# Cross-attention block on one core: the causal mask of the first two pairs laid by TensorE, and the first keys ahead of the first queries

## Chip, core and metric

The kernel runs on one core of a Trainium2 chip. The metric is the device time of one execution in microseconds. The kernel before takes 1587.69 us (median of three runs, 1587.53 to 1588.26). Engines are named as the profile names them: PE is TensorE (its weight loads are PEld), DVE is VectorE, ACT is ScalarE, POOL is GpSimd, SP is the engine that issues most DMAs. An "ACTq" or "SPq" in a view is the instruction queue of that engine where it issues a DMA.

## What is computed

For 128 sequences of 128 tokens and 256 features, in float32: queries come from `x`, keys and values from a context `c`; 16 heads of width 16; a strictly causal mask (key j is allowed for query i only if j < i); softmax; the first row of the attention set to zero; an output projection; a layer norm over the residual; a two-layer network with a hidden width of 1024 and ReLU; a second layer norm.

```python
q = (query @ Wq + bq) ; k = (key @ Wk + bk) ; v = (values @ Wv + bv)   # split into 16 heads
scores = einsum('bhqd,bhkd->bhqk', q, k) / sqrt(16)
scores = where(j < i, scores, -1e30)
attn = softmax(scores) ; attn[:, :, 0, :] = 0
x = layer_norm(query + (attn @ v) @ Wo + bo, ln1_g, ln1_b)
out = layer_norm(x + relu(x @ W1 + b1) @ W2 + b2, ln2_g, ln2_b)
```

## The kernel before

Two sequences make a pair, and 64 pairs go through the same stages. The order of instructions on each engine is written out by hand (`tc.manual_schedule`, L59): each call of a helper appends its instructions to the queues of the engines it uses, and an engine works through its queue in that order, waiting where an operand or a buffer isn't ready. `step(p)` (L799) writes the order for pair p in the middle of the kernel; the order for pairs 0 and 1 stands by itself, in L681 to L784, and there the work of these two pairs is interleaved.

The stages of a pair that matter here:

- `tokens` (L242) or, for pairs 0 and 1, `transposed` (L220) brings x and c into a layout with features on the partitions. For pairs 0 and 1 this is four TensorE transposes each, against the identity, into one bank of PSUM, which VectorE (pair 0, L689) or ScalarE (pair 1, L730) copies out.
- `queries` and `keys` (L266, L276) multiply with Wq and Wk (four matmuls of 128x128 by 256 columns) and are emptied from PSUM by ScalarE with bias and scale. Keys are written twice, once for each half of a 32-row strip (`half`, `bkh`). For pair 0 the keys are written out at L703 to L721: two banks, one emptied by ScalarE, one by VectorE.
- `scores(p, hi)` (L316): 64 small matmuls of 32 rows by 64 columns of weights. The 128 queries are split into a high half, which sees 128 keys, and a low half, which sees 64. Results stand in two tiles of two banks each, from a pool that holds two such tiles (`ps_2`, L72), so four banks in all: the next scores can be written only when the ones before have been read.
- `mask(p, hi, t)` (L340): VectorE adds the mask `neg` (0 or -1e30) to one of the two tiles and writes the sum to SBUF (`sm`). `maximum` (L352): VectorE takes the row maximum, and GpSimd subtracts it. `exponential` (L362) is ScalarE. `sums` (L368): VectorE sums and inverts, GpSimd scales.
- `turn_on_pe` (L410), for pairs 0 and 1: TensorE transposes the probabilities, four 128x128 blocks to a bank, and ScalarE copies each bank to `pT`. From pair 2 on this is done by VectorE (`turn`) and DMAs (`bring`).
- `weigh`, `context`, `attention_out`, `attention_sum`, `attention_stats`, `norm1`: probabilities times values (`pc`), output projection (`po`), residual and layer norm. `norm1(0)` is followed by TensorE transposes (`ptn`) and the hidden layer (`ph`, `py`).
- Single banks (`bank`, L213) come from a pool of four (`ps_1`, L73).

At the start, loads are issued by SP and ACT in the order of L126 to L159: the first x, Wq, Wk, Wv and so on by SP, the first c and the small bias columns by ACT. GpSimd makes the identity (L139) and the mask `neg` (L166 to L172). TensorE runs twelve transposes of the identity that nothing reads (`warm`, L681 to L683) until the first x has landed.

Of the kernel before, what the change touches and what calls it, by code (L numbers as in the profile page):

```python
# [19 lines left out]
def tile_cross_attention_block(  # L20
# [76 lines left out]
    def load_tokens(g, us=slice(0, 4)):  # L97
        if g not in tokens_of:
            tokens_of[g] = loads.tile([P, 4, D], F32, tag="x", name=f"x_{g}", bufs=2)
        nc.sync.dma_start(  # L100
            tokens_of[g][:, us], x[4 * g + us.start : 4 * g + us.stop].rearrange("b p d -> p b d")
        )


    def weight(w, name):
        n = w.shape[0] // P
        t = const.tile([P, n, w.shape[1]], F32, tag=name, name=name)
        nc.sync.dma_start(t, w.rearrange("(k p) n -> p k n", p=P))
        return t

    def column(v, name):
        t = const.tile([P, v.shape[1]], F32, tag=name, name=name)
        nc.scalar.dma_start(t, v)
        return t
# [9 lines left out]
        return t  # L124

    load_tokens(0, slice(0, 2))  # L126
    wq = weight(Wq, "wq")
    c_first = const.tile([P, 4, D], F32, tag="c_first", name="c_first")
    nc.scalar.dma_start(c_first[:, 0:2], c[0:2].rearrange("b p d -> p b d"))
    bq_c = column(bq, "bq_c")  # L130
    bk_c = column(bk, "bk_c")
    wk = weight(Wk, "wk")
    wv = weight(Wv, "wv")
    load_tokens(0, slice(2, 4))
    nc.sync.dma_start(c_first[:, 2:4], c[2:4].rearrange("b p d -> p b d"))
# [77 lines left out]
    def bank(name):  # L213
        return ps_1.tile([P, 512], F32, tag="ps1", name=name)

    def pair(name):
        return ps_2.tile([P, 2, 512], F32, tag="ps2", name=name)
# [24 lines left out]
    def tokens(p, which):  # L242
        st = states.setdefault(p, {})
        st[which + "T"] = proj.tile([P, KC, TP], F32, tag=which + "T", name=f"{which}T_{p}")
        nc.vector.transpose(
            st[which + "T"], blocks_of.pop((which, p)).rearrange("p k u f -> p k (u f)")
        )
# [18 lines left out]
    def queries(p):  # L266
        st = states[p]
        st["qT"] = proj.tile([P, KC, TP], F32, tag="qT", name=f"qT_{p}")
        pq = project(wq, st["xT"], f"pq_{p}")
        for m in range(KC):  # L270
            nc.scalar.activation(  # L271
                st["qT"][:, m, :], pq[:, m * TP : (m + 1) * TP], AF.Identity,
                bias=bqs_c[:, m : m + 1], scale=QSCALE,
            )

    def keys(p):  # L276
        st = states[p]
        st["kT"] = proj.tile([P, KC, 2, TP], F32, tag="kT", name=f"kT_{p}")
        pk = project(wk, st["cT"], f"pk_{p}")
        for m in range(KC):  # L280
            for e in range(2):
                nc.scalar.activation(  # L282
                    st["kT"][:, m, e, :], pk[:, m * TP : (m + 1) * TP], AF.Identity,
                    bias=bkh[:, m, e : e + 1], scale=half[:, e : e + 1],
                )
# [27 lines left out]

    def scores(p, hi):  # L316

        st = states[p]
        n = P if hi else HP
        sps = [pair(f"pss{hi}_{p}_{t}") for t in range(2)]  # L320
        for m in range(KC):
            for s in range(2):
                first = s * P
                for r in range(NS):
                    strip = slice(32 * r, 32 * r + 32)
                    nc.tensor.matmul(  # L326
                        sps[r // 2][
                            s * HP : (s + 1) * HP, r % 2, m * 2 * n : (m + 1) * 2 * n
                        ].rearrange("p (e j) -> p e j", e=2),
                        st["qT"][strip, m, first + hi * HP : first + hi * HP + HP],  # L330
                        st["kT"][strip, m, :, first : first + n],
                        start=True, stop=True,
                    )
        st["sps", hi] = sps
        st["sm", hi] = soft.tile(
            [P, H, n], F32, tag=f"sm{hi}", name=f"sm{hi}_{p}", bufs=2
        )
        st["nmx", hi] = small.tile([P, H], F32, tag=f"nmx{hi}", name=f"nmx{hi}_{p}")

    def mask(p, hi, t):  # L340
        st = states[p]
        part = slice(t * HH, (t + 1) * HH)
        n = P if hi else HP
        no = neg.rearrange("p u j -> p (u j)") if hi else neg[:, 1, :]
        nc.vector.tensor_tensor(  # L345
            st["sm", hi][:, part, :].rearrange("p (r n) j -> p r n j", r=2),
            st["sps", hi][t][:, :, : 4 * n].rearrange("p r (n j) -> p r n j", j=n),
            no[:, None, None, :].to_broadcast([P, 2, 4, n]),
            ALU.add,
        )  # L350

    def maximum(p, hi, part):  # L352
        st = states[p]
        n = P if hi else HP
        sm, nmx = st["sm", hi], st["nmx", hi]
        nc.vector.tensor_reduce(nmx[:, part], sm[:, part, :], AX.X, ALU.max, negate=True)  # L356
        nc.gpsimd.tensor_tensor(  # L357
            sm[:, part, :], sm[:, part, :],
            nmx[:, part, None].to_broadcast([P, part.stop - part.start, n]), ALU.add,
        )  # L360

    def exponential(p, hi, part):  # L362
        sm = states[p]["sm", hi]
        nc.scalar.activation(sm[:, part, :], sm[:, part, :], AF.Exp)  # L364
# [3 lines left out]
    def sums(p, hi, part):  # L368

        st = states[p]  # L370
        sm = st["sm", hi]
        n = sm.shape[2]
        su = small.tile([P, H], F32, tag=f"su{hi}", name=f"su{hi}_{p}_{part.start}")
        rs = small.tile([P, H], F32, tag=f"rs{hi}", name=f"rs{hi}_{p}_{part.start}")
        su, rs = su[:, part], rs[:, part]
        nc.vector.tensor_reduce(su, sm[:, part, :], AX.X, ALU.add)  # L376
        nc.vector.reciprocal(rs, su)  # L377
        nc.gpsimd.tensor_tensor(  # L378
            sm[:, part, :], sm[:, part, :],
            rs[:, :, None].to_broadcast([P, part.stop - part.start, n]), ALU.mult,  # L380
        )
# [108 lines left out]
    def attention_sum(p):  # L490
        st = states[p]
        t1 = st["t1"] = ffn.tile([P, 2, D], F32, tag="t1", name=f"t1_{p}")
        nc.vector.tensor_tensor(
            t1, st.pop("po").rearrange("p (s d) -> p s d", s=2), st.pop("xb"), ALU.add
        )
# [109 lines left out]
    def add_values(ps):  # L605
        nc.vector.scalar_tensor_tensor(bov_r, ps[:, :D], live, bo_r, ALU.mult, ALU.add)
# [72 lines left out]


    warm = bank("warm")  # L681
    for i in range(12):
        nc.tensor.transpose(warm[:, i % 4 * P : (i % 4 + 1) * P], ident, ident)  # L683
    states[0] = {}
    for which, first in (("x", tokens_of[0][:, 0:2]), ("c", c_first[:, 0:2])):
        st = states[0]
        st[which + "T"] = proj.tile([P, KC, TP], F32, tag=which + "T", name=f"{which}T_0")
        pt = transposed(first, f"pt{which}_0")
        nc.vector.tensor_copy(st[which + "T"].rearrange("p k i -> p (k i)"), pt)  # L689

    bqs_c = const.tile([P, KC], F32, tag="bqs_c", name="bqs_c")
    nc.vector.tensor_scalar(bqs_c, bq_c, QSCALE, None, ALU.mult)

    bkh = const.tile([P, KC, 2], F32, tag="bkh", name="bkh")
    for m in range(KC):
        nc.vector.tensor_scalar(bkh[:, m, :], half, bk_c[:, m : m + 1], None, ALU.mult)

    bvw = const.tile([P, KC, P], F32, tag="bvw", name="bvw")
    nc.vector.tensor_copy(bvw, bv_c[:, :, None].to_broadcast([P, KC, P]))

    queries(0)

    st["kT"] = proj.tile([P, KC, 2, TP], F32, tag="kT", name="kT_0")  # L703
    for m in range(KC):
# [16 lines left out]
                )  # L721


    scores(0, 1)
    states[1] = {}
    for which, first in (("x", tokens_of[0][:, 2:4]), ("c", c_first[:, 2:4])):
# [3 lines left out]
        nc.scalar.copy(st[which + "T"].rearrange("p k i -> p (k i)"), pt)  # L730
    values(0)
    values_out(0)
    mask(0, 1, 0)
    maximum(0, 1, ONE)
    mask(0, 1, 1)
    maximum(0, 1, TWO)
    exponential(0, 1, ONE)
    queries(1)
    scores(0, 0)
    mask(0, 0, 0)  # L740
    mask(0, 0, 1)
    maximum(0, 0, ALL)
    exponential(0, 1, TWO)
    sums(0, 1, ONE)
    keys(1)
    sums(0, 1, TWO)
    exponential(0, 0, ALL)
    values(1)
    ps_bv = fold_values()
    sums(0, 0, ALL)  # L750
    scores(1, 1)
    mask(1, 1, 0)
    add_values(ps_bv)
    maximum(1, 1, ONE)
    turn_on_pe(0, 1, range(2))
    values_out(1)
    turn_on_pe(0, 1, range(2, 4))
    mask(1, 1, 1)
    maximum(1, 1, TWO)
    add_bo(0)  # L760
    turn_on_pe(0, 0, range(2))
    tokens(2, "x")
    scores(1, 0)
    exponential(1, 1, ONE)
    weigh(0)
    context(0)
    mask(1, 0, 0)
    mask(1, 0, 1)
    maximum(1, 0, ALL)
    tokens(2, "c")  # L770
    attention_out(0)
    exponential(1, 1, TWO)
    sums(1, 1, ONE)
    attention_sum(0)
    attention_stats(0)
    exponential(1, 0, ALL)
    queries(2)
    sums(1, 1, TWO)
    keys(2)
    norm1(0)  # L780
# [254 lines left out]
```

## Time and profile before

| | us |
|---|---|
| median of three runs | 1587.69 |
| the profiled execution | 1589.6 |
| its span | 1587.9 |
| PE busy | 1574.0 (99%) |
| DVE busy | 1372.9 (86%) |
| POOL busy | 1281.9 (81%) |
| ACT busy | 757.1 (48%) |
| first matmul of the first scores / last one ends | 10.55 / 12.08 |
| first mask of pair 0 (DVE) | 12.16 |
| first transposes after the first layer norm (`ptn`) | 39.60 |
| first mask of pair 2 (DVE) | 41.40 |

Everything that follows is read from one profiled execution of 1587.9 us. A row of a timeline gives start and duration in us, then engine, line, operation, output and inputs, shape and count; in brackets stand the idle time before and what ended it. A float32 matmul is two rows there and a transpose of a float32 block is one. A row of the waits reads: who waited, for whom, how long in all, how often, the longest. A row of the windows gives the busy time of each engine in a stretch, the granted clock of TensorE, the share of the DMA engines and GB/s. A row of the groups gives busy time and mean duration in ns, and then the idle time before.

### The profile page before, as it was taken

To read this page: it belongs to the slowest core of one execution; us is meant where nothing else is said; L and a number is where in the kernel's file an instruction comes from. 1 tells how busy PE (TensorE), PEld (TensorE's weight loads), DVE (VectorE), ACT (ScalarE), POOL (GpSimd) and SP (SyncE) were. 2 spreads that over 40 slices of the span, in tenths; PEclk is the share of its full clock that TensorE was granted. 3 is DMA by queue.
4 is the path that set the end of the run, shared out by engine and by line. 5 is a ranking of instruction groups with operands and counts; after the bars stand their busy time and mean duration, and the time that the engine had idled before them with its cause. 6 is when DMAs were issued, how large, how long until landed. Compare 5 with 4: busy or idle time off the path is not lost.

```text
span 1587.9 us, 41272 instructions
## 1 busy us (share of the span) xinstructions
PE 1574.0 (99%) x16512; PEld 1327.2 (84%) x16512; DVE 1372.9 (86%) x1990; ACT 757.1 (48%) x1498; POOL 1281.9 (81%) x1104
## 2 busy tenths in 40 slices
PE   8999999999999999999999999999999999999998
PEld 6788888888888888888888888888888888888887
DVE  7999888888888988898898988888889989889872
ACT  5555445444444454454444544544444455445442
POOL 7878888788887888888888888888888888888883
PEclk9999999999999999999999999999999999999999
DMA  9555665655556556556556565565555655654521
GB/s 198 108 137 126 151 143 120 147 124 136 147 126 144 137 125 157 138 121 148 129 135 150 127 146 127 118 157 130 138 133 124 154 147 121 144 137 108 127 78 34
DMA packets 479935, 210.12 MB, mean 132 GB/s; under 512 B 348672, under 2 KB 448256, under 8 KB 479744
## 3 DMA queue, kind: packets, MB, share of 16 engines
q1 hardware_dynamic: 371104, 134.29, 38.3%
q10 hardware_dynamic: 108640, 73.19, 17.9%
q8 instruction: 131, 2.15, 0.6%
q14 instruction: 60, 0.49, 0.1%
HBM read 70.00 MB, written 33.03 MB: 65 GB/s over the span
## 4 chain that ended last, share of the span: by engine, by line
PE 92%; DVE 2%; DMA 2%; POOL 1%; SPq 1%; issue 1%; ACT 0%; ACTq 0%; POOLq 0%; DVEq 0%
PE ph L646 27%; PE py L664 26%; PE pq L260 7%; PE po L467 7%; PE pv L292 7%; PE pk L260 6%; PE pss L326 6%; PE pc L448 3%; PE pc L438 2%; DMA pT<-tb 1%; SPq L406 1%; DMA x1t<-tbx 0%; DVE sm L345 0%; DVE su L376 0%; DMA vd<-vz 0%
## 5 line engine op out<-in xcount | busy, mean ns | idle before, releaser
L357 POOL TENSOR_TENSOR sm<-sm,nmx 128x1024 f32<-128x1024 f32 x192 | 364.3, 1897 | 117.1 <-DVE nmx L356 115.3
L646 PE MATMUL ph<-x1T,w 128*128 128x256 f32 x2048 | 453.3, 379 | 0.1
L664 PE MATMUL py<-w,hT 128*128 128x256 f32 x2016 | 452.9, 382 | 0.5 <-ACT hT L652 0.4
L378 POOL TENSOR_TENSOR sm<-sm,rs 128x1024 f32<-128x1024 f32 x192 | 364.4, 1899 | 93.9 <-DVE rs L377 92.3
L664 PEld LDWEIGHTS py<-w,hT 128*128 128x128 f32 x2016 | 377.6, 190 | 73.7 <-issue 16.2
L646 PEld LDWEIGHTS ph<-x1T,w 128*128 128x128 f32 x2048 | 388.8, 190 | 53.6 <-ACT pT L423 0.5
L652 ACT ACTIVATE hT<-ph,b1e_c 128x256 f32<-128x256 f32 x504 | 209.0, 472 | 203.8 <-PE ph L646 107.9
L364 ACT ACTIVATE sm<-sm 128x1024 f32<-128x1024 f32 x192 | 200.7, 1054 | 207.9 <-POOL sm L357 199.9
L376 DVE TENSOR_REDUCE su<-sm 128x8 f32<-128x1024 f32 (+1 forms) x192 | 233.7, 1217 | 70.0 <-ACT sm L364 67.7
L345 DVE TENSOR_TENSOR sm<-pss,neg 128x1024 f32<-128x1024 f32 (+1 forms) x256 | 235.2, 939 | 48.7 <-PE pss L326 48.4
L391 DVE STREAM_TRANSPOSE tb<-sm 128x1024 f32<-128x1024 f32 x183 | 220.1, 1227 | 27.9 <-POOL sm L378 27.8
L356 DVE TENSOR_REDUCE nmx<-sm 128x8 f32<-128x1024 f32 (+1 forms) x192 | 234.3, 1220 | 6.6
L542 ACT ACTIVATE t<-t,nb,sd 128x256 f32<-128x256 f32 x124 | 67.7, 593 | 187.8 <-DMA pT<-tb 132.1
L260 PE MATMUL pq<-xT,wq 128*128 128x256 f32 x512 | 127.8, 392 | 0.0
L282 ACT ACTIVATE kT<-pk,bkh,half 128x256 f32<-128x256 f32 x252 | 120.8, 558 | 3.6 <-PE pk L260 3.6
L467 PE MATMUL po<-wo,cxT 128*128 128x256 f32 x512 | 121.1, 379 | 0.7 <-ACT cxT L460 0.7
L292 PE MATMUL pv<-wv,cT 128*128 128x256 f32 x512 | 121.0, 379 | 0.0
L260 PE MATMUL pk<-cT,wk 128*128 128x256 f32 x504 | 119.2, 379 | 0.0
L326 PE MATMUL pss<-kT,qT 32*64 32x256 f32 (+1 forms) x4096 | 116.6, 334 | 1.1 <-issue 0.7
L271 ACT ACTIVATE qT<-pq,bqs_c 128x256 f32<-128x256 f32 x128 | 53.7, 470 | 121.2 <-PE pq L260 116.5
L260 PEld LDWEIGHTS pq<-xT,wq 128*128 128x128 f32 x512 | 92.5, 190 | 20.8 <-issue 10.3
L521 POOL TENSOR_TENSOR x1b<-x,g_r 128x512 f32<-128x512 f32 x64 | 81.7, 1277 | 34.9 <-DVE x L513 34.9
(93 smaller groups left out, 1765.7 us busy)
## 6 DMA issues: line engine op xcount, KB each, us to landing
pT<-tb SPq DMA_DIRECT2D x488, 96.0 KB, 2.9
pT<-tb ACTq DMA_DIRECT2D x488, 96.0 KB, 2.7
out_dram<-t ACTq DMA_DIRECT2D x63, 256.0 KB, 2.5
xb<-in_x_dram SPq DMA_DIRECT2D x124, 128.0 KB, 4.4
cb<-in_ctx_dram SPq DMA_DIRECT2D x124, 128.0 KB, 4.3
x<-in_x_dram SPq DMA_DIRECT2D x31, 512.0 KB, 5.1
x1t<-tbx SPq DMA_DIRECT2D x248, 64.0 KB, 2.3
x1T<-x1t SPq DMA_DIRECT2D x62, 256.0 KB, 3.2
```

Of the source, the lines that this page charges most:

```text
L260: nc.tensor.matmul(ps[:, m * TP : (m + 1) * TP], w[:, k, m * P : (m + 1) * P], src[:, k, :], start=(k == 0), stop=(k == KC - 1),)
L292: nc.tensor.matmul(pv[:, s * D : (s + 1) * D], st["cT"][:, k, s * P : (s + 1) * P], wv[:, k, :], start=(k == 0), stop=(k == KC - 1),)
L326: nc.tensor.matmul(sps[r // 2][s * HP : (s + 1) * HP, r % 2, m * 2 * n : (m + 1) * 2 * n].rearrange("p (e j) -> p e j", e=2), st["qT"][str ...
L345: nc.vector.tensor_tensor(st["sm", hi][:, part, :].rearrange("p (r n) j -> p r n j", r=2), st["sps", hi][t][:, :, : 4 * n].rearrange("p r ...
L356: nc.vector.tensor_reduce(nmx[:, part], sm[:, part, :], AX.X, ALU.max, negate=True)
L357: nc.gpsimd.tensor_tensor(sm[:, part, :], sm[:, part, :], nmx[:, part, None].to_broadcast([P, part.stop - part.start, n]), ALU.add,)
L376: nc.vector.tensor_reduce(su, sm[:, part, :], AX.X, ALU.add)
L378: nc.gpsimd.tensor_tensor(sm[:, part, :], sm[:, part, :], rs[:, :, None].to_broadcast([P, part.stop - part.start, n]), ALU.mult,)
L391: nc.vector.transpose(st["tb"][:, :, at : at + 256].rearrange("p j (n a) -> p n j a", a=32), st["sm", hi].rearrange("p h j -> p (h j)")[:, ...
L467: nc.tensor.matmul(po[:, s * D : (s + 1) * D], cxT[:, k, s, :], wo[:, k, :], start=(k == 0), stop=(k == KC - 1),)
L646: nc.tensor.matmul(ph[:, i * TP : (i + 1) * TP].rearrange("p (s i a) -> p s i a", s=2, a=32), w1[:, k, (f + i) * P : (f + i + 1) * P], st[ ...
L664: nc.tensor.matmul(st["py"][:, s * D : (s + 1) * D], st["hT"][:, f, s * P : (s + 1) * P], w2[:, f, :], start=(f == 0), stop=(f == FC - 1),)
```

## The change

Five things change, all within the opening; the order from the scores of pair 2 on is the same.

1. For pairs 0 and 1 the mask is laid into PSUM by TensorE ahead of the scores (`lay`): the identity times the mask, broadcast to four copies, one matmul for each of the four score banks (512 columns in the high half, 256 in the low half). The score matmuls then add to what is there. The laying for the first scores stands right behind the warm transposes, of which four are left.
2. `mask` and `maximum` become `peak` for these two pairs: VectorE takes the maximum from PSUM and subtracts it on the way to SBUF. GpSimd subtracts nothing there.
3. The first c is transposed before the first x, and the first keys are computed before the first queries.
4. The first queries go to two banks as well, one emptied by ScalarE, one by VectorE.
5. Wk is loaded before Wq, and the column of bk before that of bq. The calls for pairs 0 and 1 are interleaved a little differently.

```diff
     load_tokens(0, slice(0, 2))
+    wk = weight(Wk, "wk")
     wq = weight(Wq, "wq")
...
+    bk_c = column(bk, "bk_c")
     bq_c = column(bq, "bq_c")
-    bk_c = column(bk, "bk_c")
-    wk = weight(Wk, "wk")
...
+    def lay(p, hi):
         n = P if hi else HP
         sps = [pair(f"pss{hi}_{p}_{t}") for t in range(2)]
+        if p < 2:
+            no = neg.rearrange("p u j -> p (u j)") if hi else neg[:, 1, :]
+            for r in range(NS):
+                nc.tensor.matmul(
+                    sps[r // 2][:, r % 2, : 4 * n].rearrange("p (n j) -> p n j", j=n),
+                    ident, no[:, None, :].to_broadcast([P, 4, n]), start=True, stop=False,
+                )
+        return sps
+
+    def scores(p, hi):
+        st = states[p]
+        n = P if hi else HP
+        sps = st.pop(("laid", hi), None) or lay(p, hi)
...
-                        start=True, stop=True,
+                        start=p >= 2, stop=p >= 2 or m == KC - 1,
...
+    def peak(p, hi, t):
+        st = states[p]
+        part = slice(t * HH, (t + 1) * HH)
+        n = P if hi else HP
+        sp = st["sps", hi][t][:, :, : 4 * n].rearrange("p r (n j) -> p r n j", j=n)
+        nmx = st["nmx", hi][:, part].rearrange("p (r n) -> p r n", r=2)
+        nc.vector.tensor_reduce(nmx, sp, AX.X, ALU.max, negate=True)
+        nc.vector.tensor_tensor(
+            st["sm", hi][:, part, :].rearrange("p (r n) j -> p r n j", r=2),
+            sp, nmx[:, :, :, None].to_broadcast([P, 2, 4, n]), ALU.add,
+        )
...
-    for i in range(12):
+    for i in range(4):
         nc.tensor.transpose(warm[:, i % 4 * P : (i % 4 + 1) * P], ident, ident)
     states[0] = {}
-    for which, first in (("x", tokens_of[0][:, 0:2]), ("c", c_first[:, 0:2])):
+    states[0]["laid", 1] = lay(0, 1)
+    for which, first in (("c", c_first[:, 0:2]), ("x", tokens_of[0][:, 0:2])):
...
-    queries(0)
...
+    st["qT"] = proj.tile([P, KC, TP], F32, tag="qT", name="qT_0")
+    for m in range(KC):
+        pq = bank(f"pq_0_{m}")
...
+        if m == 0:
+            nc.scalar.activation(
+                st["qT"][:, m, :], pq[:, :TP], AF.Identity,
+                bias=bqs_c[:, m : m + 1], scale=QSCALE,
+            )
+        else:
+            nc.vector.tensor_scalar(
+                st["qT"][:, m, :], pq[:, :TP], QSCALE, bqs_c[:, m : m + 1],
+                ALU.mult, ALU.add,
+            )
...
     values_out(0)
-    mask(0, 1, 0)
-    maximum(0, 1, ONE)
-    mask(0, 1, 1)
-    maximum(0, 1, TWO)
+    peak(0, 1, 0)
     exponential(0, 1, ONE)
+    peak(0, 1, 1)
     queries(1)
     scores(0, 0)
-    mask(0, 0, 0)
-    mask(0, 0, 1)
-    maximum(0, 0, ALL)
     exponential(0, 1, TWO)
     sums(0, 1, ONE)
+    peak(0, 0, 0)
+    peak(0, 0, 1)
+    sums(0, 1, TWO)
     keys(1)
-    sums(0, 1, TWO)
     exponential(0, 0, ALL)
     values(1)
     ps_bv = fold_values()
     sums(0, 0, ALL)
     scores(1, 1)
-    mask(1, 1, 0)
-    add_values(ps_bv)
-    maximum(1, 1, ONE)
     turn_on_pe(0, 1, range(2))
     values_out(1)
     turn_on_pe(0, 1, range(2, 4))
-    mask(1, 1, 1)
-    maximum(1, 1, TWO)
+    add_values(ps_bv)
+    peak(1, 1, 0)
     add_bo(0)
     turn_on_pe(0, 0, range(2))
+    exponential(1, 1, ONE)
+    peak(1, 1, 1)
     tokens(2, "x")
     scores(1, 0)
-    exponential(1, 1, ONE)
     weigh(0)
     context(0)
-    mask(1, 0, 0)
-    mask(1, 0, 1)
-    maximum(1, 0, ALL)
+    exponential(1, 1, TWO)
+    sums(1, 1, ONE)
+    peak(1, 0, 0)
+    peak(1, 0, 1)
+    exponential(1, 0, ALL)
     tokens(2, "c")
     attention_out(0)
-    exponential(1, 1, TWO)
-    sums(1, 1, ONE)
     attention_sum(0)
+    queries(2)
     attention_stats(0)
-    exponential(1, 0, ALL)
-    queries(2)
     sums(1, 1, TWO)
```

More of the change, by code (lines that the diff above doesn't have):

```diff
@@ L310, in values_out @@
         )
+    def lay(p, hi):
+        n = P if hi else HP
+        sps = [pair(f"pss{hi}_{p}_{t}") for t in range(2)]
+        if p < 2:
[6 more added lines that the diff above has]
+        return sps
     def scores(p, hi):
@@ L319, in scores @@
         n = P if hi else HP
-        sps = [pair(f"pss{hi}_{p}_{t}") for t in range(2)]
+        sps = st.pop(("laid", hi), None) or lay(p, hi)
         for m in range(KC):
@@ L689, in tile_cross_attention_block @@
         nc.vector.tensor_copy(st[which + "T"].rearrange("p k i -> p (k i)"), pt)
-    bqs_c = const.tile([P, KC], F32, tag="bqs_c", name="bqs_c")
-    nc.vector.tensor_scalar(bqs_c, bq_c, QSCALE, None, ALU.mult)
     bkh = const.tile([P, KC, 2], F32, tag="bkh", name="bkh")
@@ L696, in tile_cross_attention_block @@
         nc.vector.tensor_scalar(bkh[:, m, :], half, bk_c[:, m : m + 1], None, ALU.mult)
+    bqs_c = const.tile([P, KC], F32, tag="bqs_c", name="bqs_c")
+    nc.vector.tensor_scalar(bqs_c, bq_c, QSCALE, None, ALU.mult)
     bvw = const.tile([P, KC, P], F32, tag="bvw", name="bvw")
     nc.vector.tensor_copy(bvw, bv_c[:, :, None].to_broadcast([P, KC, P]))
-    queries(0)
     st["kT"] = proj.tile([P, KC, 2, TP], F32, tag="kT", name="kT_0")
@@ L721, in tile_cross_attention_block @@
                 )
+    st["qT"] = proj.tile([P, KC, TP], F32, tag="qT", name="qT_0")
+    for m in range(KC):
+        pq = bank(f"pq_0_{m}")
+        for k in range(KC):
+            nc.tensor.matmul(
+                pq[:, :TP], wq[:, k, m * P : (m + 1) * P], st["xT"][:, k, :],
+                start=(k == 0), stop=(k == KC - 1),
+            )
[8 more added lines that the diff above has]
+                ALU.mult, ALU.add,
+            )
     scores(0, 1)
```

## The prediction

> **What bounds the kernel now.** I read first the busy time by stage, since one average hides the stages.
>
> ```profile
> core 0: us, PE busy (x) PEld busy (x) DVE busy (x) ACT busy (x) POOL busy (x), PEclk, DMA share, GB/s
> 0.00:1.45 1.45, 0.00 (x1) 0.01 (x1) 0.00 (x0) 0.00 (x0) 0.78 (x8) 1.00 0.00 0
> 1.45:12.10 10.65, 10.25 (x69) 7.85 (x70) 3.17 (x9) 3.35 (x6) 4.77 (x15) 1.00 0.91 239
> 12.10:40.20 28.10, 24.76 (x326) 19.73 (x327) 26.87 (x35) 18.74 (x36) 22.95 (x14) 1.00 0.97 191
> 40.20:71.00 30.80, 29.29 (x303) 23.72 (x305) 28.60 (x35) 16.63 (x35) 26.14 (x19) 1.00 0.46 101
> 71.00:1540.00 1469.00, 1467.15 (x15522) 1238.74 (x15523) 1299.10 (x1868) 704.02 (x1390) 1207.99 (x1025) 1.00 0.58 134
> ```
>
> From 71 us on TensorE idles 1.9 us in 1469: whatever the opening loses or wins arrives at the end unchanged. The diff touches only what lies before 40.2 us (behind the softmaxes of pairs 0 and 1 all engines have the old order again). There, between 12.1 and 40.2, VectorE has 1.2 us of slack and TensorE 3.3. So the question is how late `norm1(0)` and the first mask of pair 2 come; in the trace the latter starts at 41.40. Second, the timeline of TensorE for the opening:
>
> ```profile
> 1.45 2.82 PE L683 MATMUL warm<-ident 128*128 128x128 f32 x12 [1.45 <-POOL ident masks.py:199]
> 4.27 1.12 PE L226 MATMUL ptx<-ident,x 128*128 128x128 f32 x4
> ...
> 6.17 2.41 PE L260 MATMUL pq<-xT,wq 128*128 128x256 f32 x8
> 8.41 1.89 PE L707 MATMUL pk<-cT,wk 128*128 128x256 f32 x8
> ...
> 11.39 0.69 PE L326 MATMUL pss<-kT,qT 32*64 32x256 f32 x16 [0.15 <-DVE kT L718]
> ```
>
> A projection group of eight rows (four matmuls of 256 columns, two rows each) takes 1.73 us in the chain of waits (pk, pv), so 0.216 a row; the first one, pq, takes 2.34, because its first three rows come 0.39 to 0.43 apart: up to about 7.2 us TensorE runs at half speed, though the clock column says 1.00. Third, the waits between 12 and 40.2 us:
>
> ```profile
> POOL sm L357 <- DVE nmx L356: 9.7, 4, 8.1
> PEld ptp L421 <- POOL sm L378: 3.4, 3, 1.4
> ...
> PEld ptn L226 <- DVE x L508: 0.4, 1, 0.4
> ```
>
> TensorE's one large wait there, 3.4 us of weight loads, is on GpSimd, whose line is subtract, scale, subtract, scale.
>
> **The price of a mask matmul.** No row shows one. `lay` multiplies the identity, as a 128x128 weight, by four copies of the mask: 512 columns in the high half, 256 in the low half, four matmuls each. The nearest row is the projection: 256 columns are two rows of 0.216, 0.43 us; 512 columns then 0.86, four of them 3.46, the low half 1.73. From below: an identity transpose, 128 columns in 0.108 (eight ptp weight loads in 0.86 us), would make 512 columns 0.43. From above: the half-speed row, 1.72. I take 0.86 once the clock is open, since a projection differs in no operand but its values.
>
> **The opening.** Eight transposes go (12 in 2.6 us before the pipeline's tail, so four end at 2.3). The mask is ready at 2.2 (L169 ends at 2.13). Four mask matmuls at half speed to 7.2: (7.2-2.3)/1.72 = 2.85 of them; the other 1.15 at 0.86 end at 8.2. The loads that they should cover were there before 5.0 (the weights of ptc are loaded at 4.97 without a wait), so some 3 us are not cover but delay. From there: transposes of c 8.2 to 8.9 with the tail, cT copied by DVE (0.69) to 9.6, pk 9.65 to 11.35, pq to 13.1; last query half emptied by DVE (0.53) to 13.85; the second half of the scores ends at 14.5, against 12.08. In between, what the edit wins: the last eviction is one of 0.53 us where it was two (1.00); the opening's bias columns and weights swap places in ACT's and SP's queues, and wk (5.1 us to landing) now has until 9.6, wq until 11.3. **+2.4 us.**
>
> [...]
>
> **Pairs 0 and 1, on TensorE.** Three more layings follow, none with a load to hide behind: low of pair 0, high and low of pair 1: 1.73+3.46+1.73 = 6.9 us. In exchange the subtraction leaves GpSimd: six of its 1.90 us passes (L357) go, and the 3.4 us that the transposes of probabilities waited for it. Two waits come new. The sixth group of transposes needs a bank that ACT empties after two copies, two vz copies, a DMA issue and a vd copy: it would be ready at 31.8 and gets it at 33.1; all of TensorE's line stands behind it. And the second half of `lay(1, 0)` needs the banks that `peak(1, 1, 1)` reads last: about 0.3. The schedule, issue to issue: ptx/ptc 14.35-15.2, pv 16.9, pq 18.6, lay 20.4, scores 20.9, pk 22.7, pv 24.4, ps_bv 25.2, lay 28.7, scores 29.6, five transposed groups 31.8, the sixth 33.1-33.5, lay 35.5, scores 36.1, weigh 37.5, cxT copied 38.3, po, pq, pk, pv 45.2, scores of pair 2 to 46.1. There `ptn` stands, at 39.60 before.
>
> **On VectorE.** A mask add and a maximum become a maximum and a subtraction, both from PSUM; nothing is saved:
>
> ```profile
> L356 DVE TENSOR_REDUCE nmx<-sm 128x8 f32<-128x1024 f32 x4 | 4.9, 1217 | 0.1
> L345 DVE TENSOR_TENSOR sm<-pss,neg 128x1024 f32<-128x1024 f32 x4 | 4.8, 1204 | 0.8 <-PE pss L326 0.8
> L345 DVE TENSOR_TENSOR sm<-pss,neg 128x512 f32<-128x512 f32 x4 | 2.5, 674 | 0.2 <-PE pss L326 0.2
> ```
>
> A peak of the high half is 2.4 us, of the low half 1.35. A maximum from PSUM has no row: 1.20 (L345, which reads PSUM) from below, from above the 1.90 that GpSimd takes over as many elements; I take 1.22. The subtraction likewise: L345's 1.20, at most 1.90. The shorter road to the exponential (no 1.9 on GpSimd) catches up the late start at first: the first sums of pair 0 start at about 20.0, against 19.72. Then VectorE runs dry: bov_r done at 27.4, the scores of pair 1 come only at 29.7, 2.3 us idle. From there: two peaks 34.6, xT 35.2, the exponential behind four pT copies on ACT until 36.0, sums 37.5, low peaks 40.2, cT 40.8, t and statistics 42.6, sums 43.9, norm1 (2.47, as before) 46.3, sums of the low half 47.7. First mask of pair 2: **47.7, against 41.40**. TensorE and VectorE thus arrive together, 6.3 us late. The same prices laid over the old order put that mask at 41.35.
>
> **Sum.** +2.4 at the start; +6.9 for three layings; +1.6 for the two new waits; -3.4 for the transposes' waits on GpSimd; -0.5 at `ptn`, whose later transposes waited from 39.6 to 40.1 for norm1 and now find it done; -0.7 for short stops before scores, pc and ptp (1.2 us of weight loads idle "by issue" there), which a schedule by prices alone doesn't have: **+6.3**, as VectorE's line gave. Behind it nothing is reordered, and no stage has idle time to give back. The profiled execution took 1589.6 us (span 1587.9), 1.9 above the median of 1587.7; 1589.6+6.3 = 1595.9 profiled, **1594.0** as a median.
>
> **Rivals.**
> Early clock: the half-speed rows are transposes, mostly; if it is true matmuls that open the clock, then as long after their start as in the old line (6.17 to 7.2, 1.1 us), which is 3.5. The laying then ends at 2.3+1.2+3.3x0.86 = 6.3, 1.9 earlier: +4.4, 1592.1. Against: the transposes kept TensorE just as busy.
> Dear PSUM passes: at GpSimd's 1.90 for each subtraction the schedule gives +8.9, 1596.6. Against: L345 reads PSUM at 1.20 beside a second operand.
> Cheap masks, the other side: at the transposes' 0.43 for 512 columns the start costs 0.3, the layings 3.5, and VectorE, dry no longer, decides at +2.1: 1589.8, no change. At no price at all it would be +0.2. It decides from about 0.54 us per 512 columns down (+3.2). Against: two rows per matmul, as every projection has. This is also the rival that the change does not do what it says: GpSimd is freed, and nobody was short of it but for 3.4 us.
> Faster: VectorE would have to lose work, and it loses none; the most there is to win is PE's 1.5 us of idle in 40.2 to 71.
>
> **How the numbers follow.** A measurement of this kernel can tell about 0.2%, 3.2 us, from no change. Forecast 0.65, early clock 0.10, dear passes 0.10 (all slower); cheap masks 0.11 (same); faster by some way unseen 0.04. Range: from 1590.0, just short of the cheap masks' +2.1 to +3.2, to 1597.0, past the dear passes.
>
> **What would show it.** Right: the first scores end near 14.5, L323 rows 0.43 apart, DVE waiting some 2 us for pss before the first peak of pair 1, ptn near 46, the first mask of pair 2 near 47.7, and as much at every later line. Wrong: mask rows at half that price, or a clock that opens before 4 us; a peak of over 3 us; or an end that is late by less than pair 2's mask is.

## The result

| | before | after |
|---|---|---|
| median, us | 1587.98 (5 runs, 1587.53 to 1590.45) | 1596.04 (5 runs, 1594.18 to 1596.67) |
| ratio, 95% interval | | 1.0045 [1.0030, 1.0060], +4.8 to +9.5 us |
| profiled execution / its span | 1589.6 / 1587.9 | 1596.67 / 1595.0 |
| first scores end | 12.08 | 14.52 |
| `ptn` | 39.60 | 47.48 |
| first mask of pair 2 | 41.40 | 48.39 |
| first / fifth `py` starts | 63.00 / 160.93 | 70.47 / 169.08 |

The change makes the kernel slower, by about 0.45%; 1594.0 (1590.0 to 1597.0) was forecast. `py` is the second product of the feed-forward, one per pair; but for slips in single pairs, both kernels then run at 24.26 us a pair, so its start is a good clock for comparing them. The windows of after, cut 2.4, 6.8 and 7.0 us later than those shown of before (columns as there):

```profile
1.45:14.50 13.05, 12.70 (x69) 7.52 (x69) 3.46 (x10) 2.98 (x5) 4.76 (x15) 1.00 0.96 226
14.50:47.00 32.50, 30.73 (x343) 23.60 (x348) 27.32 (x37) 18.08 (x35) 11.73 (x8) 1.00 0.77 153
47.00:78.00 31.00, 30.29 (x345) 24.32 (x333) 28.61 (x36) 16.44 (x37) 25.66 (x19) 1.00 0.48 97
78.00:1547.00 1469.00, 1466.80 (x15515) 1238.60 (x15507) 1300.31 (x1868) 706.07 (x1390) 1208.22 (x1025) 1.00 0.58 134
```

GpSimd (the fifth engine) is busy 11.73 us in the second stage, where it was 22.95. VectorE is spared nothing: 27.32 us where it had 26.87. In these windows TensorE has 6.0 us more work in a stage that is 4.4 us longer; but the cut of before lies behind the start of `ptn` and that of after ahead of it. Taken from the end of the first scores to the start of `ptn`, the stage goes from 27.52 us (24.37 busy) to 32.96 (31.19): 5.4 us longer, with 6.8 us more work and 1.4 us less idle time. The long last stage has 2.2 us of idle TensorE, where the one of before has 1.9: nothing is given back there. The timeline of TensorE after:

```profile
1.45 1.12 PE L709 MATMUL warm<-ident 128*128 128x128 f32 x4 [1.45 <-POOL ident masks.py:199]
2.35 5.95 PE L323 MATMUL pss<-neg,ident 128*128 128x512 f32 x8
8.14 0.60 PE L226 MATMUL ptc<-ident,c_first 128*128 128x128 f32 x4
...
13.18 1.34 PE L339 MATMUL pss<-kT,qT 32*64 32x256 f32 x32
...
18.83 1.89 PE L323 MATMUL pss<-neg,ident 128*128 128x256 f32 x8
...
25.69 3.60 PE L323 MATMUL pss<-neg,ident 128*128 128x512 f32 x8
...
33.74 0.66 PE L447 MATMUL ptp<-ident,sm 128*128 128x128 f32 x4 [0.93 <-ACT vd L307]
34.23 2.24 PE L323 MATMUL pss<-neg,ident 128*128 128x256 f32 x8
...
47.48 0.66 PE L226 MATMUL ptn<-ident,x 128*128 128x128 f32 x4
```

The four rows of L323 are the layings. The first one holds TensorE to 8.14, and the transposes of c start without a wait: nothing was left to cover. The third takes 3.60 us for eight records, 0.43 each; the first, with the same instructions, 5.95, because it begins at half speed (its first five rows are 0.85 apart). The waits in the second stage and the groups of the peaks:

```profile
DVE nmx L372 <- PE pss L339: 3.2, 2, 2.4
PEld pss L339 <- issue: 1.8, 4, 0.8
PEld pss L323 <- issue: 1.4, 6, 0.2
PEld ptp L447 <- ACT vd L307: 1.2, 1, 1.2
...
PEld pss L323 <- DVE sm L373: 0.5, 1, 0.5
```

```profile
L373 DVE TENSOR_TENSOR sm<-pss,nmx 128x1024 f32<-128x1024 f32 x4 | 4.9, 1224 | 0.1
L372 DVE TENSOR_REDUCE nmx<-pss 128x8 f32<-128x1024 f32 x4 | 4.9, 1219 | 3.2 <-PE pss L339 3.2
```

A wait "by issue" is time in which the engine waited for nothing that the profile shows. The wait of the transposed probabilities for GpSimd is gone. VectorE is dry for 2.4 us before the first peak of pair 1, since TensorE brings the scores late. A maximum or a subtraction from PSUM is 1.22 us.

### The profile page after: what moved, and what is told of

Its sections match the earlier page's. It is cut to its first block, busy times and chain, and to the rows that moved or that the text cites. A ratio compares the mean times of both kernels' runs of the same rounds, so it can differ in the third digit from the quotient of the medians.

```text
span 1595.0 us, 41318 instructions
## 1 busy us (share of the span) xinstructions
PE 1583.1 (99%) x16536; PEld 1331.1 (83%) x16536; DVE 1375.1 (86%) x1993; ACT 757.8 (48%) x1497; POOL 1270.8 (80%) x1098
## 4 chain that ended last, share of the span: by engine, by line
PE 90%; DVE 3%; POOL 1%; DMA 1%; ACT 1%; SPq 1%; issue 1%; ACTq 0%; POOLq 0%; DVEq 0%
PE ph L672 26%; PE py L690 25%; PE pq L260 7%; PE po L493 6%; PE pv L292 6%; PE pk L260 6%; PE pss L339 6%; PE pc L474 3%; PE pc L464 2%; DMA pT<-tb 1%; DVE su L402 1%; SPq L432 1%; PE pss L323 1%; POOL sm L383 1%; ACT sm L390 1%
## 5 line engine op out<-in xcount | busy, mean ns | idle before, releaser
L404 POOL TENSOR_TENSOR sm<-sm,rs 128x1024 f32<-128x1024 f32 x192 | 364.5, 1899 | 109.5 <-DVE rs L403 105.2
L383 POOL TENSOR_TENSOR sm<-sm,nmx 128x1024 f32<-128x1024 f32 x186 | 352.9, 1897 | 116.6 <-DVE nmx L382 114.5
L690 PEld LDWEIGHTS py<-w,hT 128*128 128x128 f32 x2016 | 377.7, 190 | 72.7 <-issue 16.2
L358 DVE TENSOR_TENSOR sm<-pss,neg 128x1024 f32<-128x1024 f32 x248 | 227.9, 940 | 55.9 <-PE pss L339 55.5
L382 DVE TENSOR_REDUCE nmx<-sm 128x8 f32<-128x1024 f32 x186 | 226.9, 1220 | 6.4
L493 PEld LDWEIGHTS po<-wo,cxT 128*128 128x128 f32 x512 | 97.2, 190 | 14.1 <-ACT cxT L486 0.9
```

The source lines that it names most:

```text
L358: nc.vector.tensor_tensor(st["sm", hi][:, part, :].rearrange("p (r n) j -> p r n j", r=2), st["sps", hi][t][:, :, : 4 * n].rearrange("p r ...
L383: nc.gpsimd.tensor_tensor(sm[:, part, :], sm[:, part, :], nmx[:, part, None].to_broadcast([P, part.stop - part.start, n]), ALU.add,)
L404: nc.gpsimd.tensor_tensor(sm[:, part, :], sm[:, part, :], rs[:, :, None].to_broadcast([P, part.stop - part.start, n]), ALU.mult,)
L493: nc.tensor.matmul(po[:, s * D : (s + 1) * D], cxT[:, k, s, :], wo[:, k, :], start=(k == 0), stop=(k == KC - 1),)
L690: nc.tensor.matmul(st["py"][:, s * D : (s + 1) * D], st["hT"][:, f, s * P : (s + 1) * P], w2[:, f, :], start=(f == 0), stop=(f == FC - 1),)
```

## The experiments

Theory: the cost is the TensorE time of the four layings; it goes to the end except where it fills a stop that TensorE had anyway, and what VectorE and GpSimd do differently is worth next to nothing. Rivals: the new order of loads and first projections is to blame; or the peaks, which hold the score banks longer. All kernels, with the offsets to the kernel before in one profiled execution each, and the time by the ratio to runs of the kernel before on the same chip (single pairs slip by up to 1.1 us within a profile, so the offset at the first `py` is the cleaner one):

| kernel | first scores end | first `py` | fifth `py` | time, us [95%] |
|---|---|---|---|---|
| after | 14.52 | +7.47 | +8.15 | +7.1 [4.8, 9.5] |
| e4: laying and peaks, old opening order | 14.03 | +6.99 | +7.48 | +7.0 [5.1, 9.1] |
| e3: new opening order alone | 11.24 | -0.84 | +0.07 | +1.3 [-0.2, 2.7] |
| e1: after without laying | 12.22 | +0.95 | +1.44 | +3.5 [1.7, 5.2] |
| e12: the same, twelve warm transposes | 11.17 | -0.13 | -0.09 | +0.2 [-1.3, 1.6] |
| e7: after, first laying left out | 11.24 | +4.14 | +5.34 | +5.4 [3.7, 7.0] |
| e2b: every laying twice | 18.06 | +17.90 | +18.19 | +18.6 [16.2, 21.1] |
| e5: layings in bfloat16 | 11.30 | +1.85 | +1.71 | +1.4 [0.0, 2.9] |
| e11: the same, one stop filled | 11.40 | +1.48 | +1.33 | +0.8 [-0.5, 2.2] |

**e1, no laying.**

```diff
-        if p < 2:
+        if False:
             no = neg.rearrange("p u j -> p (u j)") if hi else neg[:, 1, :]
...
-                        start=p >= 2, stop=p >= 2 or m == KC - 1,
+                        start=True, stop=True,
```

> The changed kernel without any laying: the four groups of mask matmuls are gone, all else (loads, order of the opening, the peaks taken from PSUM, the new order of the two first pairs) stays. The scores of pairs 0 and 1 are left unmasked, so this part of the computation is left out. Theory (the TensorE time of the four layings is the cost and passes to the end one for one, while what VectorE and GpSimd are spared gives back about 3 us of waits): 20 us of VectorE masks and GpSimd subtractions are gone and nothing stands in their place, and still the kernel is only about where the one before is, +0.2 us by the rows (first mask of pair 2 at 41.6 against 41.4), 1586.5 to 1589. The first scores end near 12.0 as before. Rival order (the loads and the opening order cost the time): it stays at 1593 to 1597, the first scores end later than 13. Rival buffers (VectorE's second pass over PSUM and the two banks that it holds set the pace): it stays above 1592, with stops of TensorE before the scores and the sixth transposed group of 3 us or more in all.

Measured 1592.16 us (7 runs), first mask of pair 2 at 41.93 (+0.53). In the trace most of the loss is gone, as the theory said; in the time half of it seems to stay, above what was expected. The opening shows a part of why: with four warm transposes and nothing behind them TensorE stood idle 2.08 us for the first c and had half-speed rows until about 7.9 us (`pk` took 2.68 us, 1.99 at full speed). e12 takes that away.

**e3, the order alone.** The kernel before, with the loads, the columns of the biases and the first projections in the order of the change; the first queries go to two banks behind the keys, as there. Nothing else is changed:

```diff
     load_tokens(0, slice(0, 2))
+    wk = weight(Wk, "wk")
     wq = weight(Wq, "wq")
...
-    for which, first in (("x", tokens_of[0][:, 0:2]), ("c", c_first[:, 0:2])):
+    for which, first in (("c", c_first[:, 0:2]), ("x", tokens_of[0][:, 0:2])):
...
-    queries(0)
...
+        pq = bank(f"pq_0_{m}")
```

> The kernel before with only the other part of the change: the weights of the keys loaded ahead of those of the queries, the first keys projected ahead of the first queries, the latter in two banks that two engines empty. Masks, maxima and subtractions as before. Theory (laying is the cost): the eviction that is shortened by one engine's turn gives 0.5 us, the time is -0.5 us, 1586.5 to 1588 beside 1587.7 of the kernel before; first scores end near 11.6, first mask of pair 2 near 40.9. Rival order: the loads in the new order come late, the first scores end 2 us later or more, and the time is 1590 or above.

Measured 1590.41 us (11 runs): not the small gain that was expected, and nothing like the rival's loss. The gain is there at first (first scores 0.84 us sooner, first mask of pair 2 at 40.55, first `py` at 62.16), and then it is lost in one place. The timeline of TensorE behind the first `py`, in the kernel before and in this one:

```profile
63.00 7.17 PE L664 MATMUL py<-w,hT 128*128 128x256 f32 x32
70.96 0.45 PE L438 MATMUL pc<-pT,vd 128*32 128x64 f32 x16 [0.79 <-DMA x1t<-tbx]
```

```profile
62.16 7.17 PE L664 MATMUL py<-w,hT 128*128 128x256 f32 x32
71.04 0.45 PE L438 MATMUL pc<-pT,vd 128*32 128x64 f32 x16 [1.71 <-DMA pT<-tb]
```

The context of pair 2 (`pc`) needs the probabilities that DMAs bring. The profile names two different transfers, but the wait ends at 71 us in both. What TensorE gains before that, it waits there. Why the transfers come no sooner in e3, whose first mask of pair 2 is 0.85 us sooner, isn't shown. In after TensorE comes to this context only at 77.58, and finds them there.

**e4, laying alone.** The changed kernel with the loads and the opening in the old order (the edits of e3 undone).

> The other half: the masks are laid by TensorE and the peaks taken from PSUM, the two first pairs in the new order, but loads and opening in the order of the kernel before (first queries ahead of first keys, one bank). Theory (laying is the cost): all of the loss is here, first mask of pair 2 near 48.4 to 48.9, the time 0.5 us above that of the changed kernel, 1594.5 to 1597.5. Rival order: 1588 to 1590.

Measured 1596.03 us (5 runs), first mask of pair 2 at 47.90: the whole loss without the new opening order. With e3 this settles that this order isn't the cause. The mask comes sooner than the 48.4 to 48.9 expected, since the first laying took 1.0 us less than after's, with the same instructions on TensorE up to there:

```profile
1.45 1.11 PE L709 MATMUL warm<-ident 128*128 128x128 f32 x4 [1.45 <-POOL ident masks.py:199]
2.36 4.95 PE L323 MATMUL pss<-neg,ident 128*128 128x512 f32 x8
```

Eight rows in 4.78 us to the next row's start, of which full-speed rows would take 3.46: about three are slow, so full speed came near 5.0 us here, and near 7.0 in after (5.79 us, 5.4 slow rows).

**e7, first laying left out.**

```diff
-        if p < 2:
+        if p < 2 and not (p == 0 and hi):
...
-                        start=p >= 2, stop=p >= 2 or m == KC - 1,
+                        start=p >= 2 or (p == 0 and hi == 1), stop=p >= 2 or (p == 0 and hi == 1) or m == KC - 1,
...
-    for i in range(4):
+    for i in range(12):
...
-    states[0]["laid", 1] = lay(0, 1)
...
-    peak(0, 1, 0)
+    mask(0, 1, 0)
+    maximum(0, 1, ONE)
+    mask(0, 1, 1)
+    maximum(0, 1, TWO)
```

> The changed kernel with three layings instead of four: the first scores of pair 0 are masked by VectorE and subtracted by GpSimd as in the kernel before, and the twelve warming transposes are back. Theory (laying is the cost): what the first laying took at half clock comes back whole, +2.4 us at the opening, of which VectorE's extra mask takes nothing, since TensorE is not waiting for it there; first scores end near 11.7, first mask of pair 2 near 45.2, time 1591 to 1593 beside 1587.7 before. Rival late clock (the first laying is free, as it lies where TensorE only warms up and waits for loads): no gain, 1594.5 to 1597, and the first scores end no sooner than 14. Rival buffers: above 1595.

Measured 1594.1 us (8 runs), a little over the range; first scores at 11.24, first mask of pair 2 at 45.06, as the theory had it. The first laying is worth 3.3 us at that mask and at the first `py`, so it isn't hidden behind loads or clock. Not all of the 3.3 is its price: TensorE was at full speed near 5.2 us in this profile (from 1 to 10 us it has e3's busy times to 0.02 us, as 1.66 us from 4 to 6 where e3 has 1.64; e3's rows are further down) and near 7.0 in after's, and in e4 such a lead was worth 1.0 us.

**e2b, every laying twice.**

```diff
-            for r in range(NS):
+            for r in range(2 * NS):
                 nc.tensor.matmul(
-                    sps[r // 2][:, r % 2, : 4 * n].rearrange("p (n j) -> p n j", j=n),
-                    ident, no[:, None, :].to_broadcast([P, 4, n]), start=True, stop=False,
+                    sps[r % NS // 2][:, r % 2, : 4 * n].rearrange("p (n j) -> p n j", j=n),
+                    ident, no[:, None, :].to_broadcast([P, 4, n]), start=r < NS, stop=False,
                 )
```

> The changed kernel with every laying made twice, the second time added to the first: the mask is twice as far below zero, the rest as it was; nothing is asked of any other engine. Theory (TensorE's layings go to the end at their price, and the waits on GpSimd that they filled are all filled by the first laying already): the three later layings cost another 1.73 + 3.46 + 1.73 = 6.9 us, the first one another 3.5 us at full clock, in all +10.0 to +10.4 us over the changed kernel, the second product of the first feed-forward at 70.5 + 10.2 = 80.7, time near 1606. Rival hidden (part of a laying still lies in the shade of VectorE's and GpSimd's work, so that it is only a few of them that cost): +3 to +7 us, 1599 to 1603. Rival clock (the first laying costs nothing, it lies where the loads and the clock are waited for): +6.9 us, 1603.

Measured 1607.92 us (4 runs); the first `py` at 80.90, 10.43 us behind after's. The second set of layings has 10.4 us of TensorE time (3.46 + 1.73 + 3.46 + 1.73), and all of it arrives. For this second set the rivals by which a laying is partly hidden fall.

**e5, layings in bfloat16.**

```diff
+    ident_h = const.tile([P, P], mybir.dt.bfloat16, tag="ident_h", name="ident_h")
+    nc.vector.tensor_copy(ident_h, ident)
+    neg_h = const.tile([P, 2, HP], mybir.dt.bfloat16, tag="neg_h", name="neg_h")
+    nc.vector.tensor_copy(neg_h, neg)
...
-                    ident, no[:, None, :].to_broadcast([P, 4, n]), start=True, stop=False,
+                    ident_h, no[:, None, :].to_broadcast([P, 4, n]), start=True, stop=False,
```

> The changed kernel with the identity and the mask kept in bfloat16 for the layings, all else as it was: each laying matmul should be one record in the place of two. No row has such a matmul; at half of the float32 price or less (0.22 to 0.43 us for 512 columns) a high laying takes 0.9 to 1.7 us in place of 3.46, a low one 0.4 to 0.9. Theory (the loss is the layings' TensorE time, and the order without any laying is already 1 to 1.4 us behind the kernel before in the trace, since VectorE and GpSimd spared do not let TensorE go on sooner): with it the loss falls from 8 us to 1.5 to 4 us, time 1589 to 1592.5, and with waits of the transposed groups on GpSimd back in part. Rival buffers or order: the price of a laying matters little, the loss stays above 5 us. Rival faster: with cheap masks the kernel beats the one before, below 1587.

Measured 1589.92 us (11 runs), in the theory's range. The third laying and the windows around a disturbance in its trace:

```profile
21.66 1.03 PE L327 MATMUL pss<-neg_h,ident_h 128*128 128x512 bf16 x4
...
28.94 0.43 PE L327 MATMUL pss<-neg_h,ident_h 128*128 128x256 bf16 x2 [0.93 <-DVE sm L377]
29.31 1.16 PE L343 MATMUL pss<-kT,qT 32*64 32x128 f32 x32
```

```profile
27.00:30.00 3.00, 1.96 (x33) 1.47 (x40) 2.48 (x4) 2.96 (x6) 0.55 (x1) 0.85 1.37 211
30.00:33.00 3.00, 2.94 (x118) 2.45 (x104) 2.86 (x5) 0.00 (x0) 1.33 (x1) 0.58 1.03 127
```

A high laying is one record per matmul and 1.03 us in place of 3.60. With most of the price gone, most of the loss goes too (+1.4 us in place of +7.1), while all else of the change is still there. In the windows the sixth figure behind the span (0.85, 0.58) is the granted clock: from about 29 to 32.5 us it was about half, and the scores took 1.16 us where they take 0.69.

**e11, one stop filled.**

```diff
-            for r in range(NS):
+            again = [0, 1] * 4 if p == 1 and not hi else []
+            for i, r in enumerate([0, 1] + again + [2, 3]):
...
-                    ident_h, no[:, None, :].to_broadcast([P, 4, n]), start=True, stop=False,
+                    ident_h, no[:, None, :].to_broadcast([P, 4, n]),
+                    start=i < 2 or r > 1, stop=False,
```

> The kernel with bfloat16 layings, and in the last laying the first two matmuls are made five times (the mask is then five times as far below zero in that half), so that TensorE has 0.9 us of work where it waited 0.93 us for the two banks that the peak of the scores before still reads. In the trace of the bfloat16 kernel the granted clock fell to about half from some 29 to 32.5 us, right behind that stop and one of 0.72 us for GpSimd, and its rows of scores and contexts took 0.66 to 1.16 where they take 0.41 to 0.69. Theory (the clock closed because TensorE did too little there): with the stop filled the clock stays open, the rows are short again, the second product of the first feed-forward comes 1.5 to 2 us sooner, at +0 to +0.4 us to the kernel before in place of +1.85, time 1588 to 1590.5, still no faster than before by more than can be told. Rival chance (the fall belongs to that one execution): the same rows are short, and the time is that of the bfloat16 kernel, 0.9 us or less from it. Rival: the clock falls all the same, +1.85 again.

Measured 1589.39 us (11 runs). The clock stayed at 1.00 and the scores took 0.69 us again, but the first `py` came only 0.37 us sooner than in e5: TensorE stopped 0.89 us in the middle of the output projection at 34.31, with no releaser in the profile. The time is in the range, the working for it isn't. And filling can't be called the cause of the open clock: e12 did even less there (1.88 us of TensorE work from 27 to 30, against 1.96 in e5) and stayed at 1.00. The rows of e11 and of e12 for that stretch, and the stop of e11:

```profile
27.00:30.00 3.00, 2.84 (x53) 2.03 (x51) 2.58 (x3) 3.00 (x6) 0.67 (x1) 1.00 1.30 240
```

```profile
27.00:30.00 3.00, 1.88 (x76) 1.30 (x77) 2.97 (x4) 1.97 (x3) 0.42 (x1) 1.00 1.33 175
```

```profile
34.31 1.02 PE L499 MATMUL po<-wo,cxT 128*128 128x256 f32 x4 [0.89 <-issue]
```

**e12, no laying, warm transposes back.** e1, and

```diff
-    for i in range(4):
+    for i in range(12):
         nc.tensor.transpose(warm[:, i % 4 * P : (i % 4 + 1) * P], ident, ident)
```

> The changed kernel without any laying, but with the twelve warm transposes of the kernel before; the scores of pairs 0 and 1 are left unmasked, so this part of the computation is left out. The kernel without laying and with four transposes idled 2.08 us ahead of its first c and had rows at half speed until about 7.9 us. Theory (the 0.95 us that it lost up to the second product of the first feed-forward is that clock, and VectorE's and GpSimd's relief is worth nothing to TensorE): its first scores end near 11.3, as with the order alone, that product comes 0.9 to 1.3 us sooner than there, between -0.4 and 0.1 us to the kernel before, time 1588 to 1590. Rival (the peaks themselves cost TensorE about a us): the opening is won, and the product still comes 0.7 us or more behind the kernel before.

Measured 1589.22 us (11 runs), as the theory had it: masks at no price, VectorE and GpSimd relieved of all that the change relieves them of, the new order of everything, and the kernel is where it was before. Its waits from 12 to 41 us show why:

```profile
PEld ptp L447 <- POOL sm L404: 2.1, 2, 1.1
...
PEld pss L339 <- DVE sm L373: 1.4, 1, 1.4
```

Of the 3.4 us that the transposed probabilities waited for GpSimd, 2.1 remain, though it subtracts nothing: it waits for VectorE's sums (`sm` L404 is the scaling behind them). And 1.4 us are new, TensorE waiting for banks that a peak still reads.

## Why the prediction was right, point by point

**What bounds.** Right for a loss: 7.0 us at the first mask of pair 2, 7.5 at the first `py`, 8.15 at the fifth, 7.1 in the span. "Unchanged" was too strong. Single pairs slip by 0.05 to 1.1 us, in both kernels and mostly not in the same pairs, which moves the offset between 8.15 and 6.15 on the way. For a gain it is wrong: e3's 0.84 us end in a wait for a transfer, at 71 us. The trace of before had 0.79 us of that wait; I read it as idle time that could be won, and it was the next bound.

**The opening, +2.4.** Measured 2.44, by the steps named: laying to 8.14 (8.2), first scores to 14.52 (14.5). The half-speed rows ended near 7.0, as the row of before (7.2) said; in e4 they ended near 5.0, which was worth 1.0 us. That the steps agree to 0.1 us is so in part by luck: nothing in the working told when they would end in this execution.

**The price of a mask matmul.** 0.86 us was right (3.60 us for four, 3.53 to the next row's start). The cheap-masks rival was right about the consequence: at no price +0.2 was worked out, -0.1 in the trace and +0.2 [-1.3, 1.6] in the time were measured (e12).

**VectorE.** The maximum 1.22 and the subtraction 1.22 as taken; 2.37 us dry, 2.3 forecast.

**The sum, +6.3: the mis-sized term is the -0.7 for short stops.** I had dropped the stops "by issue" of the old order (1.2 us of weight loads) without putting any in the new one; the new one has 1.8 before the scores and 1.4 at the layings. So TensorE falls behind the schedule by a little at most stages: scores of pair 1 at 29.22 (28.7 in the schedule), `ptn` at 47.48 (46.1). With that term at zero the sum is +7.0, which the first mask of pair 2 has. TensorE's own line has +7.5 behind `ptn` (the next transposes start at 40.50 before, at 47.98 after): 2.4 for the opening, 6.8 more work, 1.4 less idle time (3.15 to 1.77), and 0.4 less at `ptn`. Most of the other half microsecond is that waits of weight loads were taken for idle TensorE. Of the 3.4 us on GpSimd it was idle in 2.5, as the same view of before has it for PE:

```profile
PE ptp L421 <- POOL sm L378: 2.5, 3, 0.9
```

The new waits were 1.2 and 0.5 us of weight loads where 1.3 and 0.3 were taken.

**The -3.4 had the right size in weight loads and the wrong reason.** I wrote that the wait goes because the subtraction leaves GpSimd. e12 shows that this alone takes 1.3 of the 3.4 and puts 1.4 in their place. The wait went because the layings filled it: with the same peaks and order, after has neither that wait nor more than 0.5 of the 1.4. Three layings hold 6.9 us of TensorE and cost 4.3 us at the first `py` (e7 against e12, though e7 also masks its first scores in the old way; at the fifth it is 5.4, with a stop of 1.07 us in the middle of a projection at 102.79 in between), and once the stops are full, as in e2b, a laying costs its whole price.

**Left open.** e1 lost 3.5 us in time and 1.4 in its trace at the fifth `py`; e12, which differs by eight warm transposes, lost nothing. The opening accounts for 1.1 us of that; the rest falls in single pairs later (0.9 at the thirteenth) and isn't explained. Nor is the 0.67 us that after loses between the second and third `py`, where TensorE stops in the middle of a projection.

No kernel here beats the one before. e3, e5 and e11, which compute all of the output, are within 0.1% of it or a little behind.

## What to carry to other kernels

Moving work from an engine with slack to the one that sets the pace costs the work's price less the stops that it happens to fill: price it on the engine that receives it, per instruction and at that operand type, and count the stops from the trace. Before a gain is booked, look for what lands next behind the place where it is made. The cheapest test of such a change is to leave the moved work out altogether: if even that wins nothing, the relieved engines weren't the bound.

## What the runs showed of the hardware

**When TensorE reaches full speed.** TensorE's instructions were the same up to there, and it came near 5.0 us in e4 and near 7.0 in after, behind matmuls of the layings. In the kernel before it came near 7.1, behind transposes and 0.9 us of its first projection (which took 2.41 us), and near 5.2 in e3 (that projection 1.99 us), behind transposes alone:

```profile
4.53 0.94 PE L226 MATMUL ptc<-ident,c_first 128*128 128x128 f32 x4 [0.26 <-DMA c_first<-in_ctx_dram]
5.30 0.60 PE L226 MATMUL ptx<-ident,x 128*128 128x128 f32 x4
6.25 1.99 PE L706 MATMUL pk<-cT,wk 128*128 128x256 f32 x8 [0.34 <-DVE cT L689]
```

The row of `ptx`, 0.60 us where a slow one has 1.12, is at full speed with nothing but transposes before it. e7 has e3's busy times from 1 to 10 us, to 0.02 us. Over the ten profiles full speed came between about 5 us (e4) and 7.9 us (e1), by the lengths of the rows. Each kernel was profiled once, so whether it differs between executions of one kernel isn't shown here. Two runs speak against the early clock, the rival by which true matmuls bring full speed 1.1 us after their start: e3 had it with only transposes before, and after some 4.6 us behind the start of its first laying (2.35 to about 7.0).

**The clock can fall again.** In e5 it was about half for some 3.4 us (0.15 of 3 us and 0.42 of 3 us are missing from 1.00; doubled, if it was half), though no stop of TensorE in the stretch before was longer than 0.93 us. None of the other nine profiles has it there, e12 with a like pattern among them. What set it off stays open.

**A bfloat16 matmul** of 512 columns is one record, four of them 0.96 us to the next row (e5, 21.66 to 22.62); of float32 four are eight records and 3.53 us (after, 25.69 to 29.22).

**Stops in the middle of a group** of matmuls, 0.4 to 1.1 us with no releaser, came in eight places of these traces (after 81.75, 105.92 and 1514.83, e1 342.14, e4 105.14, e7 102.79, e11 34.31, before 948.82). In all but e1, where it isn't shown, the queue that the profile calls "instruction" (q8) had moved a 16 KB block 1 to 4 us earlier. That TensorE waited for its instructions there would fit, and no run tested it. Such a block alone doesn't explain a stop: the kernel before moves 131 of them, one in 12 us, and has one stop of this kind. Two more, of 0.3 us and above, stood in the groups of `pc` (e3 485.21, 0.33 us, and e11 388.60, 0.41 us).
